# Layer 0 of a four-layer graph network in fp32: attention scores from VectorE dot products or from two extra columns of the weight products

## The chip, the cores and the metric

The kernel runs on one core of a Trainium2 chip. The metric is the device time of one execution in microseconds (us). The version before the change took 5611.59 us (median of three runs, 5608.57 to 5612.69). TensorE (PE), VectorE (DVE), ScalarE (ACT), GpSimd (POOL) and SyncE (SP, which only issues transfers) work in parallel, each through its own list of instructions in order, and wait for one another by semaphores.

## What is computed

x is 128 graphs of 128 nodes with 512 features, adj a 128x128 matrix of weights for each graph (zero where there is no edge). Four layers follow each other, each as x = layernorm(x + layer(x, adj)). Layers 1 to 3 (a hypergraph convolution, a tanh attention, an eight-head attention) are not touched by the change. Layer 0, cut to its core:

```
Xw = X @ Wv + bv
sj, si = Xw @ aw[:512], Xw @ aw[512:]                 # one score of each kind a node
e  = leaky_relu(sj[None, :] + si[:, None] + ab, 0.2)
T  = A * exp(e);  T = T / (rowsum(T) + 1e-12)         # the transition matrix of the graph
H  = X @ Wk[0] + (T @ X) @ Wk[1] + (T @ T @ X) @ Wk[2] + bk (three of them)
out = relu(H)
```

The scores are linear in X, so sj = X @ (Wv @ aw[:512]) plus a constant: one vector of 512 weights for each kind of score. The kernel also uses that T acts on nodes and Wk on features: it forms Y0, Y1, Y2 = X @ Wk[0..2] and then H = Y0 + T @ (Y1 + T @ Y2).

## The kernel before

Work goes by pairs of graphs (U = 2, L27). Layer 0 takes two pairs at a time (`both`, L810), 32 times. The product of the two pairs' x with the three Wk side by side is done by Strassen's scheme in Winograd's form twice over: an outer level of seven products over the two pairs and the halves of the features (loop at L901, one of B11, B21, T2, T1, B22, T3, N4 after another), and inside each an inner level of seven (`strassen`, L536) over the two graphs and quarters. So 49 products of 128x128 by 128x384 serve two pairs. Each inner call uses three PSUM banks; the "take" functions move or add a bank into its place in R, two tiles `out` of 2 x 3 x 512 (graph, Wk, features). A quarter of the features of all three Wk is a strided view of R, three runs of 128 (`quarters`, L882). Most takes are `ve.tensor_tensor` on DVE; the first of a quarter (`fresh`, L886) copies Y1 and Y2's part on ACT and adds the bias to Y0's on DVE. POOL adds halves of R after T1 and T3 (L909 to L911) and makes all left-hand sums (L845 to L876).

The stages of a group of two pairs are the parts between two `yield`s of `layer0` (L807): load x in the blocked order that DVE's 32x32 transposition wants (`from_dram`, L811), transpose it (L816), load x once more by rows and adj (L818, L819), the scores and the softmax (L822 to L842), the left-hand sums, the products, and the tail (L914 to L930). In the scores stage, four dot products of a pair (`dot`, L447: `scalar_tensor_tensor` with an accumulated sum, written to a tile named junk) take x by rows against `wj_b` and `wi_b`, the two weight vectors spread over all partitions. Then the scores sj are spread over the partitions by PE transposes of a column (`spread_pair`, L694), ACT makes Prelu and Exp into a tile `sq`, DVE multiplies by adj and sums, POOL divides, and e goes to DRAM in eight small writes and comes back in one read (`through_dram`, L649), in whose order DVE's transposition of 32x32 blocks gives the transposed T (`pair_turned`, L701). In the tail each of two PSUM banks t0, t1 (one per graph) gets Y1 by an ACT copy, PE adds T @ Y2, ACT copies the sum back, and the same again for Y0 with T @ that sum; DVE applies relu and adds x (loaded by rows a third time, L916), and a layer norm follows (`layer_norm`, L620). The result goes to a DRAM tensor x1d.

The weights are prepared once (`prepare0`, L730). Wk's three matrices are staged in the later slots of the tile `first`, copied by ACT to W[B11], W[B21], W[B12], W[B22] (384 columns, the three Wk's quarters side by side), combined by DVE and POOL within each (`combine`, L467) and then across the seven (L759). Wv is transposed on PE, and 16 tiny products give `two`, the weight vectors of the scores as columns (L773 to L781), which PE transposes spread to `wj_b`, `wi_b` (L782, L783).

No order is written by hand. Every operation is recorded with its tiles, an estimated cost and a key (a place in the sequence, one unit for one pair); `Plan.order` (L225) simulates the five engines, gives out buffers as they come free, and lets each engine take the ready operation with the lowest key, and `emit` (L351) writes the instructions in the order of that simulation. `layer` (L1232) sets the key of a stage to the pair's number plus an offset of WHEN0, WHEN1 or WHEN2 (L35 to L37). Every instruction carries line L362, from which it is emitted, so the profile is read by the names of tiles:

- `bank<-first,four`, 128x384: a product of layer 0 (weights in `first`, a left-hand side in `four`).
- `t<-out,sq`: a tail product; `out<-bank,out`: an eviction by addition.
- `junk<-four,row`: a dot product; `sq`: softmax tiles; `e`: the trip through DRAM.
- `first<-first`: the preparation of the weights.

Of the kernel before, what the change touches and what calls it, by code (L numbers as in the profile page):

```python
# [14 lines left out]
OP = mybir.AluOpType  # L15
AX = mybir.AxisListType

P = 128
# [16 lines left out]
WHEN0 = (-3.0, -1.6, -1.5, -.5, -1.0, 0, 1.6)  # L35
# [20 lines left out]
EARLY = -0.5  # L56
SLACK = 60
SPARE, AHEAD = 3, 6
SIZE = {"four": U * D, "sq": U * (P + 2), "bank": D, "col": 12, "row": D, "w28": 7168, "w14": 3584,
        "w7": 7 * 3 * P, "out": U * 3 * D, "t0": D, "t1": D}  # L60
# [310 lines left out]
def kernel(  # L371
# [61 lines left out]
    def col(*n):  # L433
        return tile_of("col", *n)
# [15 lines left out]
    def row():  # L450
        return tile_of("row", D)
# [218 lines left out]
    def from_dram(src, kind, dmas=(sp.dma_start,)):  # L670

        nj, _, n = src.shape
        t = kind().rearrange("p u f -> p (u f)").rearrange("p (m j w) -> p m j w", m=4, j=nj)
        for j in range(nj):
            with plan.together():
                for k in range(4):
                    dmas[j % len(dmas)](t[k * Q:(k + 1) * Q, :, j],
                                        src[j].rearrange("(m r) (k w) -> k r m w", r=Q, k=4)[k],
                                        run=n // 4, parts=Q)
        return t.rearrange("p m j w -> p (m j w)")  # L680
# [36 lines left out]
    wj_b, wi_b = row(), row()  # L717
# [12 lines left out]
    def prepare0():  # L730
# [11 lines left out]
        W = WT["0"] = [tile_of("w7", 7, 1, 3 * P) for _ in range(7)]  # L742
        stage = [W[T2 + m].rearrange("p j o f -> p (j o f)")[:, :C * D].rearrange("p (c f) -> p c f", f=D)
                 for m in range(3)]
        for g in range(2):
            for m in range(3):
                with plan.together():
                    for k in range(4):
                        ac.dma_start(stage[m][k * Q:(k + 1) * Q, 2 * g:2 * g + 2],
                                     wk0[m].rearrange("(k c a) f -> k a c f", k=4, a=Q)[k][:, 2 * g:2 * g + 2],  # L750
                                     run=D, parts=Q)
        for g, half, j in ((0, 0, B11), (1, 0, B21), (0, 1, B12), (1, 1, B22)):
            to = W[j][:, :4].rearrange("p (n c) o (m i) -> p m c n (o i)", n=2, m=3)
            for m in range(3):
                ac.copy(to[:, m], stage[m].rearrange("p c (n i) -> p c n i", i=P)[
                    :, 2 * g:2 * g + 2, 2 * half:2 * half + 2])
            combine(W[j], (ve, po)[half])
        flat = [w.rearrange("p j o f -> p (j o f)") for w in W]
        for to, a, b in ((T1, B12, B11), (T2, B22, T1), (T3, T2, B11), (N4, B21, T2)):  # L759
            (po if to in (T3, N4) else ve).tensor_tensor(flat[to], flat[a], flat[b], OP.subtract)  # L760
# [6 lines left out]
        for j in range(C):  # L767
            pt = bank()
            with plan.together():
                for c in range(C):  # L770
                    pe.transpose(pt[:, c * P:(c + 1) * P], st[c // 2][:, c % 2, j * P:(j + 1) * P], ident)
            (ve.tensor_copy, ac.copy)[j % 2](wvT[j // 2][:, j % 2], pt)
# [9 lines left out]
        spread(wj_b, two[:, :, 0])  # L782
        spread(wi_b, two[:, :, 1])  # L783
# [23 lines left out]
    def layer0(i0):  # L807
# [3 lines left out]
        xbs = [from_dram(x[i:i + U], four, (sp.dma_start,) if i0 else (sp.dma_start, ac.dma_start)) for i in both]  # L811
# [5 lines left out]
        yield  # L817
        x0s = [load_rows(x[i:i + U].rearrange("b p f -> p b f")) for i in both]  # L818
        As = [load_adj(i) for i in both]  # L819
        yield  # L820
        base = plan.key
        for i, x0, A in zip(both, x0s, As):  # L822
            plan.key = base + (i - i0) * .15
            s = col(2, U)
            for b in range(U):
                dot(s[:, 0, b:b + 1], x0[:, b], wj_b)
                dot(s[:, 1, b:b + 1], x0[:, b], wi_b)
            ac.activation(s[:, 1], s[:, 1], AF.Identity, bias=c0)
            pt = spread_pair([s[:, 0, b:b + 1].to_broadcast([P, P]) for b in range(U)])
            e = sq()  # L830
            for b in range(U):
                ac.activation(e[:, b], pt[:, b * P:(b + 1) * P], AF.Prelu, bias=s[:, 1, b:b + 1], alpha=0.2)
            ac.activation(e, e, AF.Exp)
            den = col(U)
            for b in range(U):
                ve.scalar_tensor_tensor(e[:, b], e[:, b], 1.0, A[:, b], op0=OP.mult, op1=OP.mult,
                                        accum_out=den[:, b:b + 1])
            ac.activation(den, den, AF.Identity, bias=tiny)
            ve.reciprocal(den, den)
            for b in range(U):  # L840
                po.tensor_scalar(e[:, b], e[:, b], den[:, b:b + 1], None, op0=OP.mult)
            loads.append(through_dram(e.rearrange("p b (k w) -> p b k w", w=Q), f"e{i}"))  # L842
# [37 lines left out]
        R = [tile_of("out", U, 3, D) for _ in range(2)]  # L880

        def quarters(r, half):  # L882

            return [R[r][:, b, :, (2 * half + n) * P:(2 * half + n + 1) * P] for b in range(U) for n in range(2)]

        def fresh(d, bs):  # L886

            def put(d, b):
                def run(p):
                    ac.copy(d[:, 1:], p[:, 1:])  # L890
                    add(d[:, 0], p[:, 0], b, OP.add)
                return run
            d11, d12, d21, d22 = d
            return {"p1": put(d11, bs[:, 0]), "c11": lambda p: add(d11, p, d11, OP.add),
                    "v": put(d12, bs[:, 1]), "c12": lambda p: add(d12, p, d12, OP.add),
                    "p5": put(d22, bs[:, 1]), "c22": lambda p: add(d22, p, d22, OP.add),
                    "c21": put(d21, bs[:, 0])}

        C11, C12, X, Y = quarters(0, 0), quarters(0, 1), quarters(1, 0), quarters(1, 1)
        sides = [[R[r][:, b, :, h * 2 * P:(h + 1) * 2 * P] for b in range(U)] for r, h in ((0, 1), (1, 0), (1, 1))]  # L900
        for k, (j, take) in enumerate((  # L901
# [5 lines left out]
            strassen((L[:, 0, :1], L[:, 0, 1:], L[:, 1, 1:], [S[:, i:i + 1] for i in range(4)]), WT["0"][j], 1, 3 * P,  # L907
                     {n: lambda p, f=f: f(p.rearrange("p (m i) -> p m i", i=P)) for n, f in take.items()})
# [4 lines left out]
        base = plan.key  # L913
        for r, i in enumerate(both):  # L914
            plan.key = base + .4 * r
            x0 = load_rows(x[i:i + U].rearrange("b p f -> p b f"))  # L916
            TT = pair_turned(loads[r])
            for m in (1, 0):
                for b in range(U):
                    p = tile_of(("t0", "t1")[b], D)  # L920
                    t = R[r][:, b]
                    ac.copy(p, t[:, m])
                    pe.matmul(p, TT[:, b], t[:, m + 1], start=False, stop=True, skip_group_check=True)
                    if m:
                        ac.copy(t[:, m], p)
                    else:
                        ve.scalar_tensor_tensor(t[:, 0], p, 0.0, x0[:, b], op0=OP.max, op1=OP.add)
                        layer_norm(t[:, 0])
                plan.key += .2
            sp.dma_start(x1d[i // U], R[r][:, :, 0])  # L930

# [355 lines left out]
```

## Time and profile before

| | |
|---|---|
| median of three runs | 5611.59 us |
| profiled execution | 5613.66 us, its span from first to last instruction 5611.7 us |
| mean granted TensorE clock | 0.994 of full |
| busy: PE, weight load, DVE, ACT, POOL | 98%, 73%, 73%, 38%, 61% of the span |
| DMA | 683.82 MB, mean 122 GB/s |
| first and last store to x1d (layer 0's results, 64 pairs) | 125.4 and 1420.3 us |
| first product of layer 0 | 43.06 us |
| dots, 200 to 1200 us | 198, mean 985 ns |
| transfers: x by rows (512 KB) / x in blocks (64 KB) / e out / e back, 200 to 1200 us | 97 / 388 / 392 / 49, median 4.3 / 2.1 / 1.5 / 2.8 us from issue to landing |

How to read it: the page cuts the span into 40 slices of 140 us and gives each engine's busy share in tenths. Groups of instructions stand under line, engine, operation, tile written <- tiles read, and shape, with the number, the busy time, the mean duration and the idle time of the engine just before them with what ended it. An fp32 product stands as two records. The ends of products are modelled, so a mean duration of a product is longer than its share of the engine. The chain of waits follows the work that ended last back through its releasers.

### The profile page before, as it was taken

How to read it: one execution, taken by the hardware profiler on the slowest of the kernel's cores; microseconds unless marked ns; L12 is line 12 of the kernel's file. 1: busy time of each engine (PE TensorE's matmuls, PEld its weight loads, DVE VectorE, ACT ScalarE, POOL GpSimd, SP SyncE). 2: the span in 40 equal slices, each digit the busy share in tenths (PEclk: the TensorE clock that was granted, in tenths of full speed). 3: DMA queues.
4: the chain of work that ended last, by engine and by line, in shares of the span. 5: the costliest groups of instructions: out<-in, count | busy, mean ns of one | idle time of the engine just before them, and what ended most of it. 6: DMA issues, size and time to landing. Idle time of an engine off the chain costs nothing.

```text
span 5611.7 us, 88462 instructions
## 1 busy us (share of the span) xinstructions
PE 5500.8 (98%) x28705; PEld 4082.3 (73%) x28705; DVE 4076.2 (73%) x8644; ACT 2130.3 (38%) x5325; POOL 3447.4 (61%) x5076
## 2 busy tenths in 40 slices
PE   6999999999999999999999999999999999999999
PEld 3555555555666666666666798899998999999998
DVE  6999999999666656666666666767776777777766
ACT  2333334334333333333333333334333344333433
POOL 5777777776656666666566555555555555555554
PEclk8999999999999999999999999999999999999999
DMA  3444444444443333334444433344334443344442
GB/s 102 124 118 122 117 133 117 130 120 141 131 138 115 117 112 115 116 114 117 118 118 118 134 121 114 120 132 131 120 119 125 132 131 116 120 128 132 129 124 93
DMA packets 735091, 683.82 MB, mean 122 GB/s; under 512 B 260763, under 2 KB 572067, under 8 KB 734630
## 3 DMA queue, kind: packets, MB, share of 16 engines
q1 hardware_dynamic: 731014, 673.45, 40.4%
q10 hardware_dynamic: 3616, 4.72, 0.3%
q8 instruction: 228, 3.74, 0.3%
q14 instruction: 233, 1.91, 0.1%
HBM read 393.76 MB, written 284.16 MB: 121 GB/s over the span
## 4 chain that ended last, share of the span: by engine, by line
PE 77%; DVE 9%; DMA 6%; POOL 3%; issue 2%; SPq 2%; ACT 1%; DVEq 0%; ACTq 0%; POOLq 0%
PE bank L362 59%; PE t L362 18%; DVE out L362 4%; SPq L362 2%; DVE junk L362 2%; DMA four<-x 2%; POOL four L362 1%; DVE col L362 1%; DMA four<-h 1%; DMA out<-h 1%; DVE four L362 1%; POOL out L362 1%; ACT out L362 1%; DMA four<-in_x_dram 1%; POOL col L362 1%
## 5 line engine op out<-in xcount | busy, mean ns | idle before, releaser
L362 PE MATMUL bank<-first,four 128*128 128x384 f32 (+1 forms) x4904 | 1504.5, 453 | 43.8 <-DVE out L362 18.0
L362 PEld LDWEIGHTS bank<-first,four 128*128 128x128 f32 x4904 | 907.7, 191 | 589.8 <-DVE out L362 136.0
L362 DVE TENSOR_TENSOR out<-bank,out 128x384 f32<-128x384 f32 (+2 forms) x1894 | 931.4, 520 | 268.2 <-PE bank L362 251.3
L362 PE MATMUL bank<-four,four 128*128 128x256 f32 (+2 forms) x2684 | 705.0, 417 | 5.6 <-DVE out L362 2.6
L362 PEld LDWEIGHTS bank<-four,four 128*128 128x128 f32 (+1 forms) x2684 | 401.8, 176 | 242.0 <-issue 198.8
L362 ACT ACTIVATE out<-out,col,col 128x512 f32<-128x512 f32 (+1 forms) x408 | 363.7, 899 | 519.0 <-POOL col L362 505.2
L362 PE MATMUL bank<-first,out 128*128 128x256 f32 x2352 | 532.1, 379 | 0.1
L362 PEld LDWEIGHTS bank<-first,out 128*128 128x128 f32 x2352 | 441.9, 190 | 60.6 <-issue 1.0
L362 PE MATMUL bank<-four,out 128*128 128x256 f32 (+2 forms) x1856 | 482.3, 403 | 3.0 <-DVE out L362 1.4
L362 POOL TENSOR_TENSOR out<-out,row 128x512 f32<-128x512 f32 x230 | 292.5, 1277 | 309.9 <-PE bank L362 163.8
L362 POOL TENSOR_TENSOR four<-four 128x256 f32<-128x256 f32 (+2 forms) x453 | 337.4, 756 | 222.5 <-ACT four L362 164.0
L362 POOL TENSOR_TENSOR out<-out 128x768 f32<-128x768 f32 (+2 forms) x246 | 377.8, 1545 | 150.9 <-DVE out L362 105.7
L362 POOL TENSOR_TENSOR four<-four,four 128x256 f32<-128x256 f32 (+2 forms) x517 | 431.2, 838 | 28.0 <-PE bank L362 14.7
L362 DVE TENSOR_TENSOR four<-bank,four 128x256 f32<-128x256 f32 (+1 forms) x420 | 178.4, 426 | 354.7 <-PE bank L362 345.2
L362 ACT COPY four<-bank 128x256 f32<-128x256 f32 (+1 forms) x483 | 224.7, 466 | 529.5 <-PE bank L362 523.6
L362 POOL TENSOR_SCALAR col<-col 128x1 f32<-128x1 f32 (+1 forms) x704 | 195.8, 282 | 354.8 <-DVE col L362 328.0
L362 ACT COPY out<-bank 128x256 f32<-128x256 f32 (+1 forms) x464 | 183.7, 400 | 581.5 <-PE bank L362 448.7
L362 POOL TENSOR_TENSOR col<-col,neghalf 128x1 f32<-128x1 f32 x640 | 390.5, 613 | 17.8
L362 PEld LDWEIGHTS bank<-four,out 128*128 128x128 f32 (+1 forms) x1856 | 299.9, 183 | 115.9 <-issue 73.2
L362 DVE BATCH_NORM_STATS2 col<-out 128x6 f32<-128x512 f32 x492 | 334.9, 682 | 56.5 <-ACT out L362 54.4
L362 PE MATMUL bank<-out,first 128*128 128x128 f32 x2592 | 317.9, 277 | 2.9 <-DVE out L362 2.5
L362 PEld LDWEIGHTS bank<-out,first 128*128 128x128 f32 x2592 | 301.8, 192 | 11.1 <-DVE out L362 4.9
(213 smaller groups left out, 10520.8 us busy)
## 6 DMA issues: line engine op xcount, KB each, us to landing
four<-in_x_dram SPq DMA_DIRECT2D x126, 512.0 KB, 4.3
h<-out SPq DMA_DIRECT2D x336, 128.0 KB, 2.4
out<-S SPq DMA_DIRECT2D x68, 512.0 KB, 4.7
out<-h SPq DMA_DIRECT2D x66, 512.0 KB, 4.6
S<-out SPq DMA_DIRECT2D x66, 512.0 KB, 3.2
x1d<-out SPq DMA_DIRECT2D x64, 512.0 KB, 3.1
four<-in_x_dram SPq DMA_DIRECT2D x504, 64.0 KB, 2.1
four<-h SPq DMA_DIRECT2D x62, 512.0 KB, 4.8
```

What stands on the lines that cost most here:

```text
L362: call(*map(real, args), **{n: real(a) for n, a in kw.items()})
```

## The change

The two weight vectors of the scores become columns 384 and 385 of W's blocks for the first quarter of the features, so that the scores come out of the same 49 products as two more columns of quarter 0, and zeros stand in these columns for the other three quarters. A product is 386 columns wide (QW). R's layout turns from (graph, Wk, features) to (graph, quarter, 386), in which a quarter is one run. The dots, `wj_b`, `wi_b` and their spreading, and the load of x by rows for the dots are gone. The softmax moves from its own stage ahead of the products to after them, with keys of its own (WHENT: 0.8 and 2.1 units after the group's start of products for the two pairs' scores, 2.0 and 3.1 for their tails); the tail's copies and products take quarters with a step, and its result is written over x by rows. In the preparation, half of Wk's transfers are issued by SP, x's loads all by SP, the copies and sums of W come after the 16 tiny products, and Wv's transposes are written in another row order that fits Wk's.

```diff
-WHEN0 = (-3.0, -1.6, -1.5, -.5, -1.0, 0, 1.6)
+WHEN0 = (-3.0, -1.6, -1.0, 0, 0)
+WHENT = (.8, 2.1), (2.0, 3.1)
...
+QW = 3 * P + 2
...
-        "w7": 7 * 3 * P, "out": U * 3 * D, "t0": D, "t1": D}
+        "w7": 7 * QW, "out": U * 4 * QW, "t0": D, "t1": D}
...
-                        ac.dma_start(stage[m][k * Q:(k + 1) * Q, 2 * g:2 * g + 2],
+                        (ac, sp)[g].dma_start(stage[m][k * Q:(k + 1) * Q, 2 * g:2 * g + 2],
...
-        spread(wj_b, two[:, :, 0])
-        spread(wi_b, two[:, :, 1])
+        for g, half, j in ((0, 0, B11), (1, 0, B21), (0, 1, B12), (1, 1, B22)):
+            for m in range(3):
+                ac.copy(W[j][:, :4, :, m * P:(m + 1) * P].rearrange("p (n c) o i -> p c n (o i)", n=2), stage[m].rearrange("p c (n i) -> p c n i", i=P)[
+                    :, 2 * g:2 * g + 2, 2 * half:2 * half + 2])
+            scores = W[j][:, :4, 0, 3 * P:]
+            if half:
+                po.memset(scores, 0.0)
+            else:
+                po.memset(scores[:, 2:], 0.0)
+                ac.copy(scores[:, :2], two[:, 2 * g:2 * g + 2])
+            combine(W[j], (ve, po)[half])
...
-        xbs = [from_dram(x[i:i + U], four, (sp.dma_start,) if i0 else (sp.dma_start, ac.dma_start)) for i in both]
+        xbs = [from_dram(x[i:i + U], four) for i in both]
...
-        x0s = [load_rows(x[i:i + U].rearrange("b p f -> p b f")) for i in both]
-        As = [load_adj(i) for i in both]
-        yield
-        base = plan.key
-        for i, x0, A in zip(both, x0s, As):
-            plan.key = base + (i - i0) * .15
-            s = col(2, U)
-            for b in range(U):
-                dot(s[:, 0, b:b + 1], x0[:, b], wj_b)
-                dot(s[:, 1, b:b + 1], x0[:, b], wi_b)
-            ac.activation(s[:, 1], s[:, 1], AF.Identity, bias=c0)
...
-        R = [tile_of("out", U, 3, D) for _ in range(2)]
+        R = [tile_of("out", U, 4, QW) for _ in range(2)]
...
-            return [R[r][:, b, :, (2 * half + n) * P:(2 * half + n + 1) * P] for b in range(U) for n in range(2)]
+            return [R[r][:, b, 2 * half + n] for b in range(U) for n in range(2)]
...
-                    ac.copy(d[:, 1:], p[:, 1:])
-                    add(d[:, 0], p[:, 0], b, OP.add)
+                    ac.copy(d[:, P:], p[:, P:])
+                    add(d[:, :P], p[:, :P], b, OP.add)
...
+        loads = []
         for r, i in enumerate(both):
-            plan.key = base + .4 * r
+            A = load_adj(i)
+            plan.key = base + WHENT[0][r]
+            s = col(U)
+            ac.activation(s, R[r][:, :, 0, 3 * P + 1], AF.Identity, bias=c0)
+            pt = spread_pair([R[r][:, b, 0, 3 * P:3 * P + 1].to_broadcast([P, P]) for b in range(U)])
...
+        for r, i in enumerate(both):
+            plan.key = base + WHENT[1][r]
             x0 = load_rows(x[i:i + U].rearrange("b p f -> p b f"))
             TT = pair_turned(loads[r])
             for m in (1, 0):
                 for b in range(U):
                     p = tile_of(("t0", "t1")[b], D)
-                    t = R[r][:, b]
-                    ac.copy(p, t[:, m])
-                    pe.matmul(p, TT[:, b], t[:, m + 1], start=False, stop=True, skip_group_check=True)
+                    by = p.rearrange("p (q i) -> p q i", i=P)
+                    to, of = (R[r][:, b, :, k * P:(k + 1) * P] for k in (m, m + 1))
+                    ac.copy(by, to)
+                    pe.matmul(by, TT[:, b], of, start=False, stop=True, skip_group_check=True)
                     if m:
-                        ac.copy(t[:, m], p)
+                        ac.copy(to, by)
                     else:
-                        ve.scalar_tensor_tensor(t[:, 0], p, 0.0, x0[:, b], op0=OP.max, op1=OP.add)
-                        layer_norm(t[:, 0])
+                        ve.scalar_tensor_tensor(x0[:, b], p, 0.0, x0[:, b], op0=OP.max, op1=OP.add)
+                        layer_norm(x0[:, b])
                 plan.key += .2
-            sp.dma_start(x1d[i // U], R[r][:, :, 0])
+            sp.dma_start(x1d[i // U], x0)
```

The softmax's lines between (Prelu to the trip through DRAM) are the same and stand after the products now.

## The prediction

> **What bounds the kernel now.** I read the page's slices first, then stretches of the same trace, then the groups of one stretch, its waits and its chain.
>
> ```profile
> PE   6999999999999999999999999999999999999999
> DVE  6999999999666656666666666767776777777766
> ```
> The first ten slices (to about 1400 us) are layer 0, the only stage in which TensorE (PE) and VectorE (DVE) both stand at nine tenths. The busy times by stretch, of layer 0 and of layer 1, say it in numbers (us of PE, weight load, DVE, ACT, POOL; then clock, DMA share, GB/s):
>
> ```profile
> 200.00:1200.00 1000.00, 975.23 (x2865) 519.77 (x2865) 942.23 (x2227) 381.69 (x826) 750.48 (x973) 1.00 0.43 122
> 1900.00:2900.00 1000.00, 993.39 (x3809) 665.59 (x3808) 607.07 (x1196) 371.65 (x598) 607.62 (x1020) 1.00 0.40 117
> ```
> DVE has 6% to spare in layer 0 and 39% in layer 1. The groups of 200 to 1200 us by form:
>
> ```profile
> L362 PE MATMUL bank<-first,four 128*128 128x384 f32 x2383 | 822.6, 492 | 18.8 <-DVE out L362 14.0 <-ACT sq L362 1.5 <-ACT out L362 1.0
> L362 DVE TENSOR_TENSOR out<-bank,out 128x384 f32<-128x384 f32 x999 | 505.8, 544 | 32.7 <-PE bank L362 21.4 <-POOL out L362 5.4
> L362 DVE SCALAR_TENSOR_TENSOR junk<-four,row 128x512 f32<-128x512 f32 x198 | 195.0, 985 | 1.4
> L362 PE MATMUL t<-out,sq 128*128 128x512 f32 x384 | 193.6, 598 | 3.9 <-ACT t L362 3.8
> L362 DVE DVE_READ_ACCUMULATOR junk<-four,row 128x1 f32 x198 | 15.5, 78 | 0.0
> ```
> The third line is what the change removes: four dot products for each pair of graphs. PE's 492 ns for a record is modelled and overlaps; the chain of waits shows what one takes when nothing holds it:
>
> ```profile
> 818.97 22.94 PE bank L362 x72
> ```
> That is 22.94/72 = 0.3186 us a record, two records a product: 0.637 us. The stores of finished pairs (x1d) go from 125.4 to 1420.3 us, 63 steps: 20.55 us a pair. PE's own work for a pair is 24.5 products x 0.637 = 15.61, four products into t x 0.858 (12 records in 5.15 us elsewhere in the chain) = 3.43, two transposes 0.38: **19.42 us**. So 20.55 - 19.42 = 1.13 us of each pair (5.5%) is waiting, and the list of waits names whom for:
>
> ```profile
> PEld bank L362 <- DVE out L362: 105.6, 251, 5.4
> ```
> Part of those 105.6 us lies under a running product, so the gap is the smaller figure, 48.65 pairs x 1.13 = 55 us in the 1000. At most 64 x 1.13 = 72 us can be won in layer 0's steady part.
>
> The other loss is the start. PE's order of time there, with one line of ACT and one of POOL:
>
> ```profile
> 43.06 1.65 PE L362 MATMUL bank<-first,four 128*128 128x384 f32 x2 [1.70 <-ACT first L362]
> 60.47 7.48 PE L362 MATMUL bank<-first,four 128*128 128x384 f32 x14 [1.48 <-DVE first L362]
> 78.27 2.29 PE L362 MATMUL bank<-first,four 128*128 128x384 f32 x3 [10.31 <-DVE first L362]
> ```
> ```profile
> 8.85 15.48 ACTq L362 DMA_DIRECT2D first<-in_L_gnn_Wk_dram  x12
> ```
> ```profile
> 49.24 2.27 POOL L362 TENSOR_TENSOR first<-first 128x384 f32<-128x384 f32 x2 [32.00 <-ACT first L362]
> ```
> ACT issues the weights' transfers until 24.4 us, and more up to 35; their copies and sums follow, and PE has little to do until T2 exists at 78.
>
> **What the Trainium skill says.** (1) "Trainium Kernel Development and Optimization", section Performance Expectations: matmul busy time is a bad measure of distance to the limit, since matmuls are pipelined. The trace agrees: 975 of 1000 us "busy", yet 5.5% above its own work. (2) "FP8 and Floating Point Precision", TensorE Precision Notes: true fp32 takes four passes. With the 2.4 GHz that the first page gives, 384 columns x 4 is an estimate of 640 ns; the trace has 637. (3) "SBUF — State Buffer", section SBUF: two separate sides: a VectorE operation with two SBUF inputs and a GpSimd one lock each other out of a shared port. A dot has two such inputs: 0.69 us where POOL is still (37.95 to 41 us of the trace), 0.985 in layer 0. (4) "DMA: Bandwidth & Descriptors", Anatomy of one DMA: about 2 us fixed; here e is written in 1.5 us and read back in 2.8 (medians from issue to landing).
>
> **The change, part by part.**
>
> *Dots leave DVE.* Per pair 4 x (0.985 + 0.078) = 4.25 us of 19.4 (942.23/48.65). What is left, 15.1 us on a pair of about 19.8, is 76%. POOL's 128x768 sums (1.978 us here, 1.545 as mean of the page) wait less at the shared port. The cover that DVE now lacks, room to answer a finished bank at once, is what layer 1 has at 61%: there I count 36 pairs (144 records of 130 columns, four a pair) at the same 0.83 ns a column (2016 records of 256 columns x 0.2125, 1152 of 512 x 0.425, 720 short ones x 0.107) as 995 of 1000 us. Layer 0 after the change lies between that (0.5% waiting) and today (5.5%).
>
> *Two more columns.* 386 for 384: records of 384 and 512 columns cost 0.830 and 0.838 ns a column, so the price is linear: 24.5 x 2 x 1.66 ns = 0.08 us a pair, on the path. Floor 19.50 us. DVE's and POOL's 386 and 772 elements: under 0.01 us each, hidden by their idle time; if they weren't, 0.2 us a pair.
>
> *Layout by quarters.* DVE's sums write one run of 386 in place of three of 128; ACT's copies into and out of t, and the product's moving operand, become four runs of 128. No row shows this change alone. From below: the single run saves DVE perhaps 0.02 us x 20; from above: 0.05 us on each of ACT's six 512-wide copies, 0.3 us on an engine that is 38% busy, and nothing on PE. I take zero.
>
> *One load of x less.* 64 x 512 KB of 683.82 MB, and 64 issues of 0.4 us on SP: nothing waits for them (DMA share 0.43). Taken as zero, with its cover named: DMA's other half.
>
> *The scores come later.* Today the softmax chain starts from x long before its use. Now it starts from the first quarter's result and ends at the product into t. In the built program's PE order, the work between a pair's score transposes and its first product into t is 15.1 to 24 us at the rates above, in a steady pattern of about 20 and 15.8. The chain: today, from Prelu at 816.24 us to the issue of the read-back at 826.98 is 10.7 us (Prelu, Exp, two DVE products, reciprocal, POOL 1.23, eight issues on SP 3.65, landing), and to that come transposes 0.4, landing 2.8, the DVE transposition 0.43 and handing over, 0.5: **14.8 us**. So it fits, with 1 us to spare at every second pair. Queued behind it: on SP the next loads of x (prefetched one group ahead); on DVE, in order behind the transposition of the returned block, PE's evictions. From below zero (the example has 2 us of DVE queueing in it that a freer DVE takes away); from above 2 us at each second pair, 1 us a pair. I take 0.1 us a pair.
>
> *Steady sum.* 19.50, 1.2% of waiting as between the two stages (0.24), 0.1: 19.85 us; 64 x (20.55 - 19.85) = **45 us**. Range from 19.6 (61 us) to 20.35 (13 us).
>
> *The start.* Half of Wk's transfers go to SP, x's first 512 KB go first alone, and ACT issues 14 transfers in place of 34 before or among its copies. Needed before the sums: Wv, Wk and one x, 4.7 MB, at 207 to 233 GB/s (0 to 40 us): landed at about 23 us, where today the last of Wk is issued at 34.6 and lands 3.2 later. New on the path: the score columns of W wait for Wv's transposes, ACT's copies and 16 tiny products (5.7 us at half clock); these run while Wk lands, then PE's first product comes at about 28 to 30 and POOL's first sum at about 33, against 49.24. With the dots gone from DVE (seven between 43 and 76 us, some 6 us) T2's wait shrinks too. I take **18 us**, from 8 to 27; if the columns' chain ended last it would give back up to 6.
>
> *The hand-over to layer 1.* The last tails lie 0.4 to 1.1 pairs later, out tiles and W's room come free later: 0 to 12 us lost, I take 4.
>
> Sum: 45 + 18 - 4 = 59 us. The profiled execution took 5613.66 us (span 5611.7), so 5555; the median of the runs is 2 us lower, 5611.59: **5552**.
>
> **Rivals.** (a) *The chain eats part of it*: pairs at 20.2 us, start 10: 64 x 0.35 + 10 = 32, hence 5580. For it: 1 us to spare. Against: DVE waited for a returned block only 3.3 us in 1400. (b) *The chain ends last, slower*: at each second pair DVE stands before the returned block with PE's evictions behind it. Break-even is 59/32 = 1.8 us late at each, a chain of about 17.7 us; one of 19 us costs 32 x 3.2 = 102 and gives 5612 + 43 = 5655. Against it: the chain's working above, and a freer DVE shortens its queueing. (c) *Nothing to see*: PE's gaps come from the order of products within a bank, not from DVE's load, and start gains are given back: 5605. Against: the 105.6 us name DVE, and layer 1's gap is small at a lower DVE load. (d) *All of it*: pairs at 19.55, start 27: 5612 - 64 - 27 = 5521. That the dots might stay is excluded by the built program, which has none.
>
> **How the numbers follow.** Likeliest 0.62 (5552, itself 5532 to 5572), (a) 0.22, (b) 0.08, (c) 0.04, (d) 0.04. The range leaves out (b), (c), half of (d) and the end of (a): 5527 to 5592. A measurement here can tell 0.2% (11 us) from no change; faster by more than that: 0.62 + 0.22 + 0.04 less a tail, 0.87; same 0.04; slower 0.09.
>
> **What would show it.** x1d's stores 19.8 to 19.9 us apart; DVE near 0.76 busy from 200 to 1200 us, the wait of weight loads for DVE's out well under half of 105.6; no long wait of DVE for the read of e; first product before 32 us and T2's before 65. Wrong if DVE or PE waits for e's block or for ACT's sq by more than 1 us a pair, if 386-column records take over 0.325 us in a long run, or if the first product comes after 40 us.

## The result, and the profile after

The changed kernel took 5560.67 us (median of four runs, 5559.29 to 5564.81), the kernel before 5610.08 us on the same chip (four runs, 5606.61 to 5612.69): a ratio of 0.9914, with an interval from 0.9896 to 0.9931, or 49.4 us less. The profiled executions took 5560.11 and 5613.66 us, 53.5 apart.

The slices of the page, and then the two stretches that the prediction looked at (us of PE, weight load, DVE, ACT, POOL; clock, DMA share, GB/s):

```profile
PE   8999999999999999999999999999999999999999
...
DVE  6888888878666666666665666767677777776766
```
```profile
200.00:1200.00 1000.00, 993.56 (x2951) 533.92 (x2950) 804.46 (x1876) 385.50 (x851) 716.77 (x1000) 1.00 0.35 100
1900.00:2900.00 1000.00, 995.20 (x3822) 668.82 (x3822) 607.34 (x1195) 373.71 (x600) 613.08 (x1030) 1.00 0.40 116
```
DVE's nines of layer 0 have become eights, 942 us of 1000 have become 804, and the same stretch holds more matmuls (2951 records for 2865). The groups of 200 to 1200 us, by form:

```profile
L364 PE MATMUL bank<-first,four 128*128 128x386 f32 x2451 | 843.0, 491 | 6.4 <-ACT out L364 3.6 <-DVE out L364 0.8
L364 DVE TENSOR_TENSOR out<-bank,out 128x386 f32<-128x386 f32 x1025 | 538.6, 549 | 157.0 <-PE bank L364 107.1 <-POOL out L364 33.3 <-DVE out L364 0.3
L364 PE MATMUL t<-out,sq 128*128 128x512 f32 x400 | 200.6, 593 | 0.0
L364 POOL TENSOR_TENSOR out<-out 128x772 f32<-128x772 f32 x100 | 182.3, 1831 | 174.3 <-DVE out L364 154.3 <-DVE col L364 18.8 <-ACT out L364 1.2
```
The idle time ahead of PE's products (18.8 us before) is 6.4; DVE's sums now stand idle 157 us, two thirds of it for PE; and the dots have no line. The waits of the same stretch:

```profile
PEld bank L364 <- DVE out L364: 92.2, 237, 1.1
...
DVE sq L364 <- DMA sq<-e: 0.3, 1, 0.3
```
The second line answers the rivals (a) and (b), in which the late scores hold the pairs up: DVE waited for a returned e once, 0.3 us. The start, in PE's order of time and then ACT's transfers:

```profile
26.95 4.23 PE L364 MATMUL bank<-first,four 128*128 128x386 f32 x6 [0.94 <-ACT first L364]
...
53.17 7.81 PE L364 MATMUL bank<-first,four 128*128 128x386 f32 x14 [2.10 <-DVE first L364]
```
```profile
1.88 15.46 ACTq L364 DMA_DIRECT2D first<-in_L_gnn_Wk_dram  x12
```
The first product comes at 26.95 us (before 43.06), T2's at 53.17 (before 78.27).

**Where the time went.** Products of layer 0 can be counted in the trace: half the records of the form bank<-first,four of 384 or 386 columns, 24.5 to a pair, 64 pairs. Four marks divide the gain:

| profiled execution | products by 200 us | in 200 to 1200 us | us a pair | last product of layer 0 | end of span |
|---|---|---|---|---|---|
| before | 157 | 1191.5 | 20.56 | 1390.9 | 5611.7 |
| after | 185 | 1224.5 | 20.01 | 1343.1 | 5558.2 |

By 200 us the changed kernel is 28 products ahead; at 0.64 us each that is 17.9 us. From there about 56.5 pairs are left, 0.55 us faster each: 31 us. The two make 49; layer 0's last product came 47.7 us earlier. The other 5.8 us of the span came after that product, nearly all of it in layers 1 to 3, whose operations are the same and stand in another order; no run takes that part by itself.

### The profile page after: what moved, and what is told of

Read it like the earlier page. It is cut to its first block, busy times and chain, and to the rows that moved or that the text cites. A ratio compares the mean times of both kernels' runs of the same rounds, so it can differ in the third digit from the quotient of the medians.

```text
span 5558.2 us, 87851 instructions
## 1 busy us (share of the span) xinstructions
PE 5489.4 (99%) x28697; PEld 4082.3 (73%) x28697; DVE 3872.5 (70%) x8130; ACT 2121.4 (38%) x5327; POOL 3370.9 (61%) x5080
## 4 chain that ended last, share of the span: by engine, by line
PE 85%; DMA 4%; DVE 4%; POOL 2%; issue 1%; SPq 1%; ACT 1%; DVEq 0%; ACTq 0%; POOLq 0%
PE bank L364 66%; PE t L364 19%; DVE out L364 2%; SPq L364 1%; DMA four<-x 1%; POOL four L364 1%; DMA four<-h 1%; DMA out<-h 1%; DVE col L364 1%; DVE four L364 1%; POOL out L364 1%; POOL col L364 1%; ACT out L364 1%; DVE sq L364 0%; DMA four<-in_x_dram 0%
## 5 line engine op out<-in xcount | busy, mean ns | idle before, releaser
L364 PE MATMUL bank<-first,four 128*128 128x386 f32 (+1 forms) x5372 | 1614.5, 447 | 21.7 <-DVE first L364 5.1
L364 DVE TENSOR_TENSOR out<-bank,out 128x386 f32<-128x386 f32 (+2 forms) x1785 | 913.6, 531 | 491.1 <-PE bank L364 423.5
L364 PE MATMUL bank<-four,four 128*64 128x128 f32 (+3 forms) x2508 | 598.1, 399 | 0.0
L364 POOL TENSOR_TENSOR out<-out 128x772 f32<-128x772 f32 (+2 forms) x212 | 330.3, 1564 | 255.4 <-DVE out L364 214.7
L364 PEld LDWEIGHTS bank<-four,four 128*128 128x128 f32 (+2 forms) x2508 | 338.5, 172 | 188.2 <-issue 155.0
L364 POOL TENSOR_TENSOR four<-four,four 128x256 f32<-128x256 f32 (+2 forms) x566 | 447.1, 792 | 10.7
L364 PE MATMUL bank<-four,first 128*128 128x128 f32 x3536 | 422.3, 275 | 0.7 <-DVE four L364 0.7
L364 PEld LDWEIGHTS bank<-four,first 128*128 128x128 f32 x3536 | 414.4, 192 | 7.1 <-DVE four L364 1.1
L364 PE MATMUL bank<-first,out 128*128 128x256 f32 (+1 forms) x1748 | 407.5, 380 | 0.5 <-DVE out L364 0.3
L364 PE MATMUL bank<-four,out 128*128 128x512 f32 (+3 forms) x1500 | 402.8, 416 | 2.6 <-DVE four L364 2.6
L364 PE MATMUL bank<-out,four 128*128 128x256 f32 (+3 forms) x1768 | 363.0, 363 | 8.2 <-DVE out L364 6.2
```

The source lines that it names most:

```text
L364: call(*map(real, args), **{n: real(a) for n, a in kw.items()})
```

## The experiments

Theory A, of which the expectations speak: it is the time of the dots on DVE, and at the start the earlier weights, that PE had been waiting for. Against it stood that the second load of x was what mattered (its four-tile buffers, its place in SP's queue), that e's trip had become a limit of its own, and that it was mostly the order that the planner happened to make. Each kernel is compared with the kernel before on the same chip; the last three columns are of profiled executions, as above. The kernel before took 5610.04 to 5610.49 us on the chips of the result and of e1 to e8, and 5606.96 us on that of e9 to e12. Where one of these four is set against the changed kernel, the difference of the medians is therefore some 3 us uncertain.

| kernel | us (median) | ratio to before, interval | products by 200 us | us a pair | last product of layer 0 |
|---|---|---|---|---|---|
| after | 5560.67 | 0.9914 (0.9896 to 0.9931) | 185 | 20.01 | 1343.1 |
| e1_dots_back | 5628.83 | 1.0035 (1.0022 to 1.0048) | 169.5 | 20.8 | 1406.4 |
| e2_load_back | 5568.32 | 0.9927 (0.9912 to 0.9942) | 184 | 20.1 | 1353.2 |
| e3_before_short_dots | 5622.10 | 1.0024 (1.0014 to 1.0033) | 160.5 | 20.9 | 1407.4 |
| e4_before_new_start | 5606.32 | 0.9989 (0.9980 to 0.9997) | 149 | 20.1 | 1384.5 |
| e5_before_order_short_dots | 5571.69 | 0.9928 (0.9911 to 0.9945) | 167.5 | 20.0 | 1351.0 |
| e6_load_back_order_full_dots | 5771.23 | 1.0283 (1.0268 to 1.0299) | 156 | 23.3 | 1555.4 |
| e7_before_start_short_dots | 5622.95 | 1.0023 (1.0015 to 1.0031) | 162.5 | 20.9 | 1404.5 |
| e8_before_slack50 | 5620.12 | 1.0019 (1.0013 to 1.0026) | 160.5 | 20.8 | 1408.2 |
| e9_after_slack50 | 5565.78 | 0.9926 (0.9911 to 0.9940) | 181 | 20.1 | 1356.5 |
| e10_after_order_wk_by_act | 5572.89 | 0.9940 (0.9925 to 0.9954) | 174.5 | 20.0 | 1352.0 |
| e11b_bufs13_rows6 | 5572.86 | 0.9941 (0.9924 to 0.9957) | 186 | 20.2 | 1352.6 |
| e12_after_dve_cost | 5532.62 | 0.9868 (0.9853 to 0.9882) | 193.5 | 19.7 | 1322.4 |

### The dots and the load put back into the changed kernel

e1 brings the load of x by rows and the four dots of a pair back at their old place; their results go nowhere. e2 is the same with dots of 8 columns. In both the scores still come from the two columns.

```diff
-WHEN0 = (-3.0, -1.6, -1.0, 0, 0)
+WHEN0 = (-3.0, -1.6, -1.5, -.5, -1.0, 0, 0)
...
+        x0s = [load_rows(x[i:i + U].rearrange("b p f -> p b f")) for i in both]
...
+                dot(s[:, 0, b:b + 1], x0[:, b, :512], wj_b[:, :512], 512)      # e2: 8 in place of 512
+                dot(s[:, 1, b:b + 1], x0[:, b, :512], wi_b[:, :512], 512)
```

> The changed kernel, with the four dot products of 512 for each pair and their load of x by rows put back at their old place; their results are used by nothing (the scores still come from the two columns). If VectorE's time for the dots is what made a pair 20.55 us in place of 20.0, pairs go back to 20.4 to 20.6 us and the time to about 5592 us (5585 to 5605), the start kept. If the layout by quarters or the smaller start made the gain, it stays near 5561 us (5556 to 5570).

> As e1_dots_back, but each dot product takes 8 columns in place of 512: the load of x by rows and the instructions are back, VectorE's time is not. If the dots' time is the cause: 5563 us (5558 to 5570). If the third load of x (33.5 MB, 64 issues on SyncE) is the cause, both this run and e1_dots_back stand near 5590 us.

e2 is 7.6 us above the changed kernel by medians: the cost of the load, of the short dots that remain and of the change of order, together. e1 is 60.5 us above e2, and 0.35% above the kernel before, which has the same dots. So it lost more than was expected, and more than the dots cost there. Some 10 us of it lie in the start (169.5 products by 200 us, 185 in the changed kernel):

```profile
87.98 4.20 PE L364 MATMUL bank<-first,four 128*128 128x386 f32 x6 [20.84 <-DVE out L364]
```
PE stood still for 20.84 us, a stall that neither kernel has. The rest lies in the pace, 20.8 us a pair. The direction is theory A's; the size is not.

### The dots alone taken from the kernel before, planned anew

e3 shortens the dots of the kernel before to 8 columns (98% of each score's sum is left out; e, the softmax and all that follows stay); the planner counts them as 8 columns and makes its own order.

```diff
-                dot(s[:, 0, b:b + 1], x0[:, b], wj_b)
-                dot(s[:, 1, b:b + 1], x0[:, b], wi_b)
+                dot(s[:, 0, b:b + 1], x0[:, b, :8], wj_b[:, :8], 8)
+                dot(s[:, 1, b:b + 1], x0[:, b, :8], wi_b[:, :8], 8)
```

> The kernel before, with dot products of 8 columns in place of 512 (98% of the scores' sum is left out). If VectorE's time for the dots is the cause of the slower pairs, these go from 20.55 to about 20.0 us, and with some 4 us less at the start: 5572 us (5564 to 5580). If layout or order made the gain: 5600 to 5610 us.

This fell: 12 us slower than the kernel before instead of 38 faster. DVE had less to do and PE waited more. The stretch of 200 to 1200 us of e3, and its waits:

```profile
200.00:1200.00 1000.00, 962.31 (x2826) 512.50 (x2824) 875.24 (x2182) 374.18 (x816) 688.29 (x962) 1.00 0.42 121
```
```profile
PEld bank L362 <- DVE out L362: 102.7, 173, 1.7
PEld bank L362 <- ACT out L362: 38.9, 48, 1.9
PE bank L362 <- DVE out L362: 23.4, 42, 1.1
```
DVE 875 us for 942, and PE 962 for 975. Waits for ACT's takes stand at 38.9 us, where the kernel before has 10.7. Two groups of DVE tell part of it:

```profile
L362 DVE SCALAR_TENSOR_TENSOR sq<-sq,sq 128x128 f32<-128x128 f32 x96 | 77.8, 828 | 18.7 <-ACT sq L362 18.7
...
L362 DVE SCALAR_TENSOR_TENSOR junk<-four,row 128x8 f32<-128x8 f32 x192 | 62.8, 327 | 3.6
```
In this order the softmax's products take 828 ns each, in the kernel before 432. Two of them in a pair give 0.8 us of the saving back, and DVE's busy time falls only from 19.4 to 18.3 us a pair.

### The new start alone in the kernel before, and both parts without the columns

e4 gives the kernel before the new order of the first transfers (half of Wk's to SP, x whole by SP); e7 is e3 and e4 together. Both are planned anew.

```diff
-                        ac.dma_start(stage[m][k * Q:(k + 1) * Q, 2 * g:2 * g + 2],
+                        (ac, sp)[g].dma_start(stage[m][k * Q:(k + 1) * Q, 2 * g:2 * g + 2],
...
-        xbs = [from_dram(x[i:i + U], four, (sp.dma_start,) if i0 else (sp.dma_start, ac.dma_start)) for i in both]
+        xbs = [from_dram(x[i:i + U], four) for i in both]
```

> The kernel before, with half of Wk's transfers issued by SyncE and all of x's by SyncE, as in the changed one, and nothing else. If the start's gain of some 18 us comes from the weights landing earlier, the first product comes near 30 us and the time falls by 10 to 18 us, to about 5596 us. If it comes from the dots that no longer stand on VectorE between 38 and 76 us, or from the order of the sums, it falls by less than 5 us.

> The kernel before with both the new split of the weights' transfers (as in e4) and dot products of 8 columns (as in e3; 98% of the scores' sum is left out), planned anew. If these two parts make the gain together, the start gains some 18 us and pairs take 20.0 us: about 5565 us (5555 to 5575). If the softmax after the products and the layout by quarters are needed, or if the order is a matter of luck: 5595 us or above.

e4's first product came at 32.27 us instead of 43.06, but at 200 us it was 8 products behind the kernel before, and the whole was only 3.7 us faster; by its expectation (under 5 us) that spoke against the weights' transfers. Its later pairs went at 20.1 us, with the same dots and 948 us of DVE in the 1000: an order that was better by 0.46 us a pair with nothing taken out of DVE's work. e7 missed as e3 did. So two kernels whose plans differ do not tell what one cost is worth: the plan itself moves the time by as much.

### How much the order alone is worth

e8 and e9 change only a constant of the planner in the kernels before and after: how many ns later than the soonest an operation may start and still be taken for its lower key.

```diff
-SLACK = 60
+SLACK = 50
```

> The kernel before, with the planner's SLACK of 60 ns set to 50: the same work in an order that differs in its ties. It shows how far the order alone moves the time. Theory A: within 5 us of 5610. Theory B: 10 us or more away, on either side.

> The changed kernel with the planner's SLACK of 60 ns set to 50: the same work in an order that differs in its ties, as e8 was for the kernel before (which got 10 us slower). If the changed kernel's gain is a lucky order, it moves by 10 us or more; if VectorE's spare time makes the order matter less, it stays within 5 us of 5560.7.

The same work in another order: 9.6 us more for the kernel before, 5.1 us more for the one after by medians (8 us, if each is taken against the kernel before on its own chip). Both fall between the two ranges that were expected. One constant in two kernels gives a size of the scatter, not its limit; e4's pairs show more. It also says that the gain of 49 us doesn't hang on one order of the changed kernel: e9 keeps 41 of it on its own chip (5606.96 to 5565.78).

### The same order, only the durations changed

e5 is the kernel before, instruction for instruction in its own order, since the planner counts the dots with 512 columns as before; what is executed reads 8 columns (98% of each score's sum is left out). e6 goes the other way: e2's order, planned with dots of 8 columns, executed with 512.

```diff
+    def dot0(dst, u, v):
+        def call(to, a, s, b, **kw):
+            nc.vector.scalar_tensor_tensor(to[:, :8], a[:, :8], s, b[:, :8], **kw)
+        plan.add(DVE, call, "scalar_tensor_tensor", (junk[:, :512], u, 1.0, v), dict(op0=OP.mult, op1=OP.mult, accum_out=dst))
...
-                dot(s[:, 0, b:b + 1], x0[:, b], wj_b)
-                dot(s[:, 1, b:b + 1], x0[:, b], wi_b)
+                dot0(s[:, 0, b:b + 1], x0[:, b], wj_b)
+                dot0(s[:, 1, b:b + 1], x0[:, b], wi_b)
```

> The kernel before with every instruction in its place and order, but each of layer 0's dot products takes 8 columns when it runs (98% of the scores' sum is left out), while the planner still counts 512. Only VectorE's time changes, by about 4 us a pair. Theory A, VectorE's time for the dots holds the pairs up: pairs from 20.55 to 20.0 us or less and the start some 5 us shorter, about 5572 us (5560 to 5585). Theory B, the order that the planner writes out sets the pairs' time and VectorE's load hardly matters: 5600 to 5610 us.

> e2_load_back with every instruction in its place and order, but each dot product takes all 512 columns when it runs, while the planner counts 8; the results are not used. Theory A: pairs from 20.1 to 20.5 us or more, since the order leaves no room for the dots: 5600 us or above (5595 to 5640). Theory B: 5570 to 5580 us.

e5 lands on theory A's number: 38.8 us faster than the kernel before, with one thing changed. Its stretch of 200 to 1200 us, the group of its dots and its waits:

```profile
200.00:1200.00 1000.00, 990.25 (x2955) 542.06 (x2954) 871.75 (x2288) 392.98 (x853) 720.34 (x1008) 1.00 0.43 125
```
```profile
L452 DVE SCALAR_TENSOR_TENSOR junk<-four,row 128x8 f32<-128x8 f32 x201 | 84.3, 419 | 1.4
```
```profile
PEld bank L362 <- DVE out L362: 58.2, 162, 3.5
```
Two things are to be seen. An 8-column dot still takes 419 ns on average where a full one took 985, so only 4 x 0.57 = 2.3 us a pair left DVE, about half of the 4.25 us that the change removes, and that was enough for nearly the same pace (19.97 us a pair for 20.01). And e3, which shortens the same dots, is 50 us slower: its order takes 18.3 us of DVE for a pair, e5's 17.4, and PE waits more in it. What e5 doesn't separate is the way by which the dots held PE up: POOL's sums of 128x768 became shorter too, from 1978 to 1814 ns. The chain of waits from 200 to 1200 us points to DVE: it ran over DVE's evictions and dots for 13.0% and 7.6% of the stretch in the kernel before, and for 2.8% and 1.7% in e5; POOL's `out` and `four` had 2.0% and 1.7% before.

e6 shows the reverse, and it is far steeper than expected: 203 us above e2. Its stretch of 200 to 1200 us, and its waits:

```profile
200.00:1200.00 1000.00, 897.02 (x2529) 484.54 (x2530) 831.14 (x1952) 333.13 (x729) 665.30 (x858) 0.94 0.38 108
```
```profile
PEld bank L364 <- DVE out L364: 152.2, 124, 6.0
PE bank L364 <- DVE out L364: 104.7, 31, 5.3
```
In an order made without room for the dots PE waits for DVE's results up to 6.0 us at a time, and with those pauses the mean granted clock of PE is 0.94 in the stretch. The 203 us are thus no price of the dots, which is e5's 38.8; they come with durations that the order doesn't know, and the lower clock is in them.

### The weights' transfers alone

e10 has the changed kernel's order, with all of Wk's transfers issued by ACT, as before, in place of half of them by SP.

```diff
+        by_act = lambda *args, **kw: plan.add(SP, nc.scalar.dma_start, "dma_start", args, kw)
+        move = ac.dma_start, by_act
...
-                        (ac, sp)[g].dma_start(stage[m][k * Q:(k + 1) * Q, 2 * g:2 * g + 2],
+                        move[g](stage[m][k * Q:(k + 1) * Q, 2 * g:2 * g + 2],
```

> The changed kernel with every computing instruction in its place and order, but all of Wk's transfers issued by ScalarE, as before the change (the planner counts them as SyncE's). ScalarE then issues 12 more transfers before its copies. If the weights' earlier arrival makes the part of the start's gain that the dots don't explain (28 products ahead at 200 us, against 10.5 in e5), this costs 8 to 14 us: about 5571 us. If the order of the sums made it, under 3 us.

As expected: 12.2 us above the changed kernel (15 us, if each is taken against the kernel before on its own chip). ACT's transfers, and PE's first product in this kernel:

```profile
1.86 26.92 ACTq L364 DMA_DIRECT2D first<-in_L_gnn_Wk_dram  x20
```
```profile
38.46 3.63 PE L364 MATMUL bank<-first,four 128*128 128x386 f32 x6 [0.87 <-ACT first L364]
```
ACT is busy with these issues until 28.8 us where the changed kernel lets it go at 17.3, its copies come that much later, and the first product by 11.5 us. The loss stays to the end. With e5's 38.8 us this makes 51 for the 49.4 us measured; that is near, but the two were measured in different orders, so it isn't a proof that nothing else counts.

### What is left, and a better version

In the changed kernel a pair takes 20.01 us and PE's own work, as the prediction counts it, 19.50, though DVE is busy only 80%. Windows of 10 us in the changed kernel:

```profile
828.00:838.00 10.00, 10.00 (x29) 4.99 (x28) 5.27 (x13) 2.70 (x6) 7.62 (x8) 1.00 0.32 81
838.00:848.00 10.00, 10.00 (x31) 5.60 (x30) 8.02 (x18) 1.87 (x5) 5.57 (x4) 1.00 0.57 170
848.00:858.00 10.00, 10.00 (x31) 5.17 (x30) 9.80 (x24) 6.30 (x14) 6.48 (x14) 1.00 0.15 54
858.00:868.00 10.00, 9.58 (x31) 5.19 (x29) 9.51 (x23) 3.49 (x9) 8.99 (x16) 1.00 0.31 79
868.00:878.00 10.00, 9.82 (x28) 5.21 (x29) 5.50 (x14) 3.59 (x8) 7.43 (x8) 1.00 0.67 179
```
DVE swings between 5.3 and 9.8 of 10 within the 40 us of two pairs. Cut into windows of 10 us, the stretch of 200 to 1200 us has one in each 40 us, 25 in all, in which DVE is 97 to 99% busy. 20 us as full as those from 848 on (96 to 98%) come in every second 40 us; in the others the fullest 20 us stand at 90 and 91%. In this fullest part the chain of waits runs over DVE and not over PE (start, us, what):

```profile
847.83 1.72 PE t L364 x4
849.55 1.96 PE bank L364 x6
...
852.00 0.85 DVE four L364
...
855.57 0.52 DVE four L364
...
859.95 1.47 DVE out L364 x3
...
864.15 1.17 DVE out L364 x3
...
868.18 1.56 PE bank L364 x4
```
Transpositions of the next x (four), evictions and the tails bunch there. Two attempts followed. e11b gives the plan one more `four` buffer for loads ahead, and takes two of the eight `row` buffers for it; e12 brings the planner's estimates nearer to what DVE takes: it counts 67 + 386/0.96 = 469 ns for an eviction that takes 549 in the trace, and e12 makes every estimate for DVE 12% larger. Nothing else of either kernel changes.

```diff
-BUFS = 12
+BUFS = 13
...
-ROWS = 8
+ROWS = 6
```
```diff
-        return 67 + n / (1.92 if fast else .96) + (61 * scalars if n > 8 else 0)
+        return 1.12 * (67 + n / (1.92 if fast else .96) + (61 * scalars if n > 8 else 0))
```

> The changed kernel with 13 buffers of kind four in place of 12, paid for with two of the eight rows. In the changed kernel VectorE is full (95%) for some 20 us of every 40, among other things because both transpositions of the next x fall in that half; if they wait for a buffer there, a thirteenth spreads them and pairs go from 20.0 towards 19.6 us: 5545 us (5535 to 5560). If the order of the products sets that stretch, 5561 us within 8.

> The changed kernel with the planner's costs of VectorE raised by 12% (it counts 467 ns for an eviction of 384 columns, the traces show 520 to 549). If the waits that are left come from an order that trusts in a faster VectorE than there is, pairs go to about 19.8 us and the later layers gain too: 5548 us (5535 to 5560). If not, 5561 us, 10 either way.

e11b missed: 12.2 us more than the changed kernel, so this exchange doesn't pay; as it also takes rows away, it doesn't tell what room for loads alone is worth. e12 took 5532.62 us, a ratio of 0.9868 to the kernel before, 28 us (0.5%) under the changed kernel by medians (25 us, if each is taken against the kernel before on its own chip): faster than both, and by more than expected. Its stretches, four of its 10-us windows, and its wait:

```profile
200.00:1200.00 1000.00, 997.90 (x2993) 552.30 (x2992) 840.24 (x1905) 397.51 (x866) 729.64 (x1020) 1.00 0.35 100
1900.00:2900.00 1000.00, 999.78 (x3853) 676.61 (x3853) 612.26 (x1209) 372.90 (x607) 624.50 (x1038) 1.00 0.42 118
```
```profile
840.00:850.00 10.00, 10.00 (x34) 5.80 (x33) 9.53 (x22) 1.85 (x4) 8.05 (x12) 1.00 0.21 54
850.00:860.00 10.00, 9.92 (x30) 5.28 (x29) 7.92 (x22) 6.49 (x15) 6.34 (x10) 1.00 0.64 178
860.00:870.00 10.00, 10.00 (x32) 5.61 (x30) 7.91 (x16) 1.34 (x3) 5.19 (x7) 1.00 0.31 88
870.00:880.00 10.00, 10.00 (x31) 5.40 (x30) 8.41 (x23) 5.98 (x14) 9.13 (x14) 1.00 0.26 98
```
```profile
PEld bank L364 <- DVE out L364: 12.5, 51, 0.3
```
DVE is busier in the same stretch (840 us for 804, 16.6 us a pair for 16.1), and yet PE's weight loads wait for its sums 12.5 us instead of 92.2. In these windows it lies between 7.9 and 9.5; over all hundred of the stretch between 6.7 and 9.5, where the changed kernel has 5.1 to 9.9. Of the 28 us, layer 0's last product gives 20.7 by the profiled executions. The rest comes from the later layers, where PE goes from 995.2 to 999.8 of 1000 in layer 1. One factor was tried. The waits agree with the cause that e12 was built on, but e4's order was better by as much with nothing less to do, so it isn't shown that the truer durations, and not just another order, made the gain.

## Why the prediction was right, and where it was off

**The mechanism.** "Dots leave DVE" and "the start" are both shown with the order held fixed: 38.8 us (e5) and 12.2 us (e10). That DVE, 94% busy, set PE's gaps through its late answers is what e5 supports: only the dots' duration was changed in it, and the chain of waits moved off DVE's evictions and dots. This holds for the order of the kernel before. How much of the changed kernel's pace comes from its own new order isn't shown, since e4's order reached 20.1 us a pair with all the dots in it. The total came out nearer than its terms: the steady sum was 15 us too large and the hand-over 10 us too small, and that they offset each other is luck.

**The start** was forecast at 18 us and came to 17.9, with the first product before 32 us and T2's before 65, as written. Two parts of it can be told: e5, without new transfers, is 10.5 products ahead of the kernel before at 200 us (6.7 us from DVE), and e10 is 10.5 products behind the changed kernel (6.7 us by 200 us, 12.2 at the end). That leaves 7 of the 28 products, 4.5 us, for the new order of the start and what else changed there.

**The steady sum** was too large: 45 us forecast, 30 measured (47.7 less the start's 17.9). Two terms of it failed. First, the count: the prediction multiplied by all 64 pairs, though the first 7.5 lie within the start's 18 us; 56.5 pairs x 0.70 would have been 39.6. Second, the waiting, taken as 0.24 us a pair "as between the two stages", with 0.1 for e's chain: the measured pair is 20.01 less 19.50, so 0.51. The chain's part is nearly nothing (0.3 us in 1000). Most of the gap is waiting for DVE: weight loads stood 92.2 us for its sums, 26 us for ACT's copies, partly under running products. The step that failed is the scale from layer 1: it set PE's gap by DVE's mean load. The mean of 80% hides 10 us at 97 to 99% in every 40. In e12 half of the gap is gone (19.74 us a pair) with DVE not less busy but more.

**The two columns** were put at 0.08 us a pair. No run speaks against it: 44 records of 386 columns took 13.91 us, 0.316 us each, under the 0.325 that was to be the sign of an error. They weren't tried alone; e5 without them makes 19.97, but in another order. The layout by quarters was taken as zero; no run tries it by itself.

**DVE** was forecast at 76% and 15.1 us a pair; it was 80% and 16.1. The instructions did what was forecast: the number of each group times its mean, summed, fell from 22.5 to 18.2 us a pair, by 4.3. But busy time counts overlapping records once, and the overlap shrank by 1.0 us a pair, which is the whole error. One group shows it: 999 sums of 544 ns, 543 us, stood in 505.8 us of busy time before, and 1025 of 549 ns, 563 us, in 538.6 after. Taking a sum of instructions off a busy time mixed two measures. POOL's sums waited less, as forecast: 1831 ns for 772 columns after, 1978 for 768 before. The 1545 ns that the prediction sets beside this is a mean over three shapes, not of this one.

**The hand-over to layer 1** was forecast as a loss of 4 us; the rest of the kernel gained 5.8 in the profiled execution. The last tails did lie later, as forecast: the last store of x1d came only 36.0 us earlier (1384.3 for 1420.3), the last product 47.7; the later layers made that good. Another order does as much as the 5.8: what follows layer 0's last product took 4215.1 us in the changed kernel and 4210.1 in e9.

**Two signs that missed.** The stores of x1d were to come 19.8 to 19.9 us apart. By the prediction's own measure, from the first (108.4 us) to the last, they came 20.25 apart (20.55 before), since the last ones lie that late; the products' 20.01 from 200 to 1200 us is the better measure of the pace. And the weight loads' wait for DVE was to be well under half of 105.6 us. It was 92.2, while PE's gap fell from 1.13 to 0.51 us a pair. The wait of a weight load counts also while a product still runs, as the prediction itself said; what fell was the longest one, 5.4 us to 1.1. The first page of the Trainium skill (Trainium Kernel Development and Optimization, Performance Expectations), on which the prediction leaned, held further: PE's busy share said 99.4% of the stretch where the work itself is 97.5% (19.50/20.01).

**The rivals.** (a) and (b), e's chain, fall by the 0.3 us. (d) asked for 19.55 us a pair. (c), that order and not load makes the gaps, is half right, though its number was not: SLACK alone moves these kernels by 5 to 10 us (e8, e9), and e12's order gave 28. What e3's plan does badly is settled only in part: its longer softmax products give back 0.8 us a pair of DVE's time, but why PE waits more than before, with DVE still less busy, stays open.

## What to carry to other kernels

Where a planner or scheduler writes the order, test a cost with the order held fixed, by planning with the old duration and executing another: e3 and e5 shorten the same dots and differ by 50 us in the result. Judge whether an engine has room in windows shorter than one period of the work, since a mean of 80% hid 10 us at 97 to 99% in every 40 here. And try the planner with the durations of the trace under load: with 12% more on one engine's estimates it made an order that is 28 us faster, about half of what the whole change gave.

## What was not expected of the hardware

A dot of 8 columns with an accumulated sum took 419 ns on average in e5, 327 in e3 and 197 in e2. The mean hides two cases. Of 17 such dots of e5 between 800 and 880 us, twelve took 0.13 to 0.17 us. The five longer ones, up to 1.73 us, ended when one of POOL's additions did. Lines of DVE and of POOL:

```profile
855.39 1.73 DVE L452 SCALAR_TENSOR_TENSOR junk<-four,row 128x8 f32<-128x8 f32 x1
...
862.16 0.17 DVE L452 SCALAR_TENSOR_TENSOR junk<-four,row 128x8 f32<-128x8 f32 x1
```
```profile
853.51 3.58 POOL L362 TENSOR_TENSOR out<-out 128x768 f32<-128x768 f32 x2 [0.32 <-DVE out L362]
```
The dot of 1.73 us ended at 857.12, POOL's second addition at 857.09. e3's softmax products show the same: one of 1.89 us from 803.78 on, with two such additions of POOL until 805.52. So in these kernels the length of such an operation of DVE depends on what the order puts beside it on POOL.

The granted PE clock, 1.00 in every other stretch shown here, was 0.94 in e6, where PE waited for up to 6.0 us at a time. And issuing transfers took longer at the start of the kernel than the 0.4 us for each that the prediction counted on SP: ACT's 20 weight transfers took 26.92 us in a row (1.35 us each), 12 of them 15.46 us (1.29 each), and the 12 that SP issues in the changed kernel 10.42 us (0.87 each).
